# A four-layer graph network: rows of edge weights fed to TensorE between windows, and layer 1 regrouped as 6, 7, 6, 6

## The chip, the cores and the metric

The kernel runs on one core of a Trainium2 chip. The metric is the device time of one execution in microseconds; the time of the kernel before is the median of three runs.

## The reference

A graph of 3125 nodes with 128 features and 103,125 edges sorted by destination goes through four layers, each followed by a residual and a layer norm. Cut to what the change touches, layers 0 and 1:

```python
# layer 0: weighted sum over edges
xw = x @ weight
out = relu(segment_sum(edge_val[:, None] * xw[src], dst, N) + b)
x = layernorm(x + out)

# layer 1: four heads of attention over the edges, and a loop on each node
h = (x @ W).reshape(n, 4, 32)
e = leaky_relu(a_s[src] + a_d[dst], 0.2)
p = exp(e - segment_max(e, dst)[dst])
out = segment_sum(h[src] * (p / z[dst])[:, :, None], dst, n)   # z = segment_sum(p, dst)
out = layernorm_with_gain(out.reshape(n, 128) + gat_bias + x @ skip_W + skip_b)
x = layernorm(x + out)
```

Layer 2 is an attention over the edges with one head, layer 3 two mean aggregates with matrices. Both read the counts of edges that the first stage makes.

## The kernel before, in words

The edges are turned into two dense matrices in device memory once: `wd`, the sums of edge weights (float32, source by destination, read by rows), and `f_ctd`, the counts of edges (bf16, read by all later layers). The nodes are 25 blocks of 128, the sums over edges then matrix products. Only `fast_path` runs here; a general path stands behind a flag.

*Edge stage (`make` L827, loop L871 to L931).* The edges are cut into windows of 5 nodes each; 16 windows make a batch of 80 nodes, and there are 40 batches, of which the last has 4 windows. For the next batch VectorE makes the one-hot matrices `ohd` and `ohc` (L849) and the weighted `wod` (L860, the weight in three bf16 parts); ScalarE makes part of the third (`more`, L866). For each four windows of the batch TensorE then makes 8 products of counts (`cp`, L893) and 24 of weights (`wp`, L901) in two PSUM tiles of a three-bank pool (tag "cw"); ScalarE copies them out to `cs` (L906) and `ws` (L912), with four of its own scalings for the next batch between (`cur[3](k)`). At the batch's end SyncE issues two stores of `ws` to `wd` (L914), after every odd batch one of `cs` to `f_ctd` (L917).

*Keys (`keys_of` L659).* Every eighth batch (b % 8 == 2, while batches 8 to 32 are ahead) the edges' columns are turned by six TensorE transposes into two tiles of the same three banks, and copies by ScalarE and VectorE (L537, L539, L694, L697, L698) spread them from there; the banks are held until the last has read them.

*Rows of layer 0 (`add0` L801, `while` L927).* After batch 2, whenever a row block of 128 sources is complete in `wd` by stores a batch older, SyncE issues two loads of half a row, 640 KB each (`cw`, L807, pool `f_zp` of three tiles), and TensorE runs 20 float32 products of it (L811) into five PSUM banks that hold the first 20 destination blocks. Rows that aren't done at the end of the loop follow after it (L930). A scheduler orders each engine's instructions over the whole stage, by its own costs and the priorities of the source's order; nothing is fixed by hand.

*Before layer 1 (L1188 to L1209).* The remaining five destination blocks are summed from all 25 rows (pool `tp`), and between the rows stand the attention scores of the first 20 blocks (`scores1`), their factors, and every third row from row 13 on the values of two blocks (`values`, L1158 on).

*Layer 1 (L1198 to L1349).* The destinations are taken in groups of blocks, `IG` (L503), with two heads at a time; such a sweep goes over the 25 chunks of sources. A chunk's counts are loaded, and two masks are made: one in five by VectorE alone (L1249), the others by ScalarE (`fm`, L1255) and VectorE (`cm`, L1256). For each block of the group TensorE runs three products (L1266, L1271) into the block's own PSUM bank. After a sweep VectorE sums the parts (`sums`, L1290), GpSimd and VectorE form the quotients (L1296 to L1312). Other work is hung between the chunks by `later` and `step`: the skip products (`skips`, L1276 to L1280), norms (`finish1`, L1039), the turned features for layer 2 (`turn2`, L1009 to L1020). They take their PSUM tile from `bank()`, which is one bank named "few" here, beside seven banks for the group's blocks. In group 0 other work is hung as well: the scores and factors of blocks 20 to 24 and the rest of the values.

Of the kernel before, what the change touches and what calls it, by code (L numbers as in the profile page):

```python
# [7 lines left out]
F32 = mybir.dt.float32  # L8
# [493 lines left out]
GM = 40.0  # L502
IG = [(0, 4), (4, 7), (11, 7), (18, 7)]  # L503
QG = [(0, 13), (13, 12)]
# [6 lines left out]
def fast_path(  # L511
# [146 lines left out]

    def keys_of(g):  # L659

        eg = egs[g]
        kd2 = kp.tile([P, P // BW, 2, BW, 2], BF16, name="kd2")
        kc2 = kp.tile([P, P // BW, 2, BW, 2], BF16, name="kc2")
        w2 = [kp.tile([P, P // BW, 2, BW, 2], BF16, name=f"w2_{s}") for s in range(3)]
        kic = ep.tile([P, EW], F32, name="kic", bufs=2)
# [5 lines left out]
        kid = ep.tile([P, EW], F32, name="kid", bufs=2)  # L671
        nc.vector.tensor_copy(kid.rearrange("p (a k) -> p a k", k=16), eg[:, :, 1, :])
        wei = ep.tile([P, EW], F32, name="wei", bufs=2)
# [12 lines left out]
        def pairs(i, h):  # L686
            return each(i, h)[:, :, :, None].to_broadcast([P, P // BW, BW, 2])

        wt = ep.tile([P, 2, P], F32, name="wt", bufs=2)
        wu = kp.tile([P, 2, P], F32, name="wu")  # L690
        for h in range(2):
            copy(kd2[:, :, h, :, :], pairs(t0, h))
            copy(kc2[:, :, h, :, :], pairs(t0[:, 2:, :], h))
            nc.scalar.copy(w2[0][:, :, h, :, :], pairs(t1, h))  # L694
        for s, (i, o) in enumerate(((t1, wt), (wt, wu))):
# [6 lines left out]
    keys = {0: keys_of(0)}  # L702


# [55 lines left out]
    def xw_of(b0, n):  # L760

        t = zps.tile([P, 512], F32, name="trx", tag="acc0")
        for k in range(n):
            nc.tensor.transpose(t[:, k * P : (k + 1) * P], x[:, b0 + k, :], ident)
        xT = ep.tile([P, 512], F32, name="f_xTb", bufs=2)
        nc.scalar.copy(xT[:, : n * P], t[:, : n * P])
# [33 lines left out]

    def add0(pool, i, accs, blocks):  # L801

        b0, n = blocks
        for h in range(0, n, 10):
            m = min(10, n - h)
            cw = pool.tile([P, min(10, n), P], F32, name="cw")[:, 0:m]
            nc.sync.dma_start(  # L807
                cw.rearrange("p c d -> p (c d)"), wd[i * P : (i + 1) * P, (b0 + h) * P : (b0 + h + m) * P]
            )
# [61 lines left out]
    acc0 = None  # L871
    done = 0
    cur = make(0)
    with tc.issue_after(tip[0].ins), tc.issue_after(tip["keys"].ins):
        keys[1] = keys_of(1)
    for k in range(0, BW, 4):
        cur[3](k)
    for b in range(NBT):
# [8 lines left out]
        for k in range(0, nw, 4):  # L887
# [22 lines left out]
            if cur and (b + 1 < NBT - 1 or k < LW):  # L910
                cur[3](k)
            nc.scalar.copy(ws[:, k : k + 4, :], wp)  # L912
        for a, e in ((0, 112), (112, KW)):
            nc.sync.dma_start(wv_[b * BW : b * BW + nw, a:e, :].rearrange("w k d -> k w d"), ws[a:e, 0:nw, :])  # L914
# [6 lines left out]
        if b == 2:  # L921
# [158 lines left out]
    with ExitStack() as st:  # L1080
# [29 lines left out]
        def scores1(g):  # L1110

            b0, n = GB[g]
            tag = f"acc{min(g, 2)}"
            turned(zps, xT, b0, n, tag)
            for k in range(n):
                b = b0 + k
                nc.tensor.matmul(
                    t8[:, b * 2 * H : (b + 1) * 2 * H], xT[:, b * P : (b + 1) * P], watt, start=True, stop=True
                )
            t = zps.tile([P, 512], F32, name="tr_ad", tag=tag)  # L1120
            nc.tensor.matmul(t[0:H, : n * P], watt[:, H:], xT[:, b0 * P : (b0 + n) * P], start=True, stop=True)
# [3 lines left out]

        def heads(b0, n):

            b = slice(b0, b0 + n)
            nc.vector.tensor_copy(
                sa[:, b, :], t8[:, b0 * 2 * H : (b0 + n) * 2 * H].rearrange("p (b h) -> p b h", h=2 * H)  # L1130
            )
            nc.vector.tensor_scalar(nas[:, b], sa[:, b, 0:H], -1.0, None, OP.mult)
            nc.gpsimd.tensor_scalar(bas[:, b], sa[:, b, 0:H], UP, None, OP.mult)
# [48 lines left out]
        def top():  # L1182
            heads(0, Z0)
            ex = fp.tile([P, H], F32, name="ex", bufs=1)
# [99 lines left out]
        def sums(acc, g, hp):  # L1284
# [462 lines left out]
```

## Time and profile before

| what | us |
|---|---|
| median of three runs (1521.67 to 1522.70) | 1522.51 |
| the profiled execution | 1520.03 |
| its span in the profile | 1518.2 |
| edge stage with rows, 90.0 to 467.5 | 377.5 |
| rows left after it, 467.5 to 500.0 | 32.5 |
| last five blocks of layer 0 and scores, 500.0 to 543.5 | 43.5 |
| layer 1, 543.5 to 953.5, four groups in two sweeps each | 410.0 |
| layer 1's end and layer 2, to 1249 | 295.5 |
| layer 3, to 1518.2 | 269.2 |

The profiled execution is 1.83 us longer than its span, and 2.48 shorter than the median. In the profile's lines an engine is PE (TensorE), PEld (its weight loads), DVE (VectorE), ACT (ScalarE), POOL (GpSimd) or SP (SyncE); "SPq" is SyncE's issuing. A row of the table by stage reads: from:to and length, then for each engine its busy time and, in brackets, its instructions, then TensorE's granted clock as a share of full speed, the busy share of the 16 DMA engines, and the rate in GB/s. A row of waits reads: the engine, what waits and at which line, what released it, the total in us, how often, and the longest. A group of instructions reads: line, engine, operation, result and operands with their shapes, how many; then busy time in us and the mean of one in ns; then idle time just before them and what ended it. Ends of products are modelled, so the step from one product's start to the next one's is the safer measure of its cost.

### The profile page before, as it was taken

The page shows a single profiled execution, that of the slowest core. Times are in us where ns is not written, and L with a number is a line of the kernel's source. Part 1 is how long each engine was busy: PE and PEld are TensorE (multiplying, and loading weights), DVE is VectorE, ACT ScalarE, POOL GpSimd, SP SyncE. Part 2 cuts the span into 40 slices and gives each one's busy share as a digit, 9 for nine tenths or more (in the row PEclk, how much of TensorE's full clock was granted, in tenths as well). Part 3 has the DMA queues.
Part 4 walks back from the last instruction along what each step waited for, and adds up shares of the span by engine and source line. Part 5 has one row for each costly group of instructions (what it writes and reads, how often), then busy time and mean ns, then how long its engine had stood idle before and what let it go on. Part 6 is the DMA issues. An engine that isn't in the chain of part 4 may idle for free. (4 is left out here: it accounts for less than half of the span.)

```text
span 1518.2 us, 35039 instructions
## 1 busy us (share of the span) xinstructions
PE 1386.5 (91%) x14762; PEld 1214.1 (80%) x14775; DVE 979.0 (64%) x1619; ACT 905.9 (60%) x1847; POOL 129.9 (9%) x163
## 2 busy tenths in 40 slices
PE   4898999999998987899989989899999999999995
PEld 3798999899898876889979979677777774458995
DVE  4999999989990489879968878544465352012006
ACT  2988887878882479878778677454465331023003
POOL 1000000000000023203212311300000000000000
PEclk9999999999999999999999999999999999999997
DMA  7378887877889633444434433332222218513541
GB/s 204 93 182 230 217 221 191 245 196 207 230 229 254 214 93 98 144 124 123 129 116 120 130 92 105 119 115 68 69 60 80 76 58 301 197 43 131 197 154 46
DMA packets 209734, 223.92 MB, mean 147 GB/s; under 512 B 72988, under 2 KB 183371, under 8 KB 209309
## 3 DMA queue, kind: packets, MB, share of 16 engines
q1 hardware_dynamic: 208780, 218.51, 49.7%
q8 instruction: 117, 1.92, 0.5%
q0 software_dynamic: 400, 1.97, 0.4%
q10 hardware_dynamic: 385, 1.11, 0.2%
q14 instruction: 52, 0.43, 0.1%
HBM read 157.19 MB, written 64.36 MB: 146 GB/s over the span
## 5 line engine op out<-in xcount | busy, mean ns | idle before, releaser
L1271 PE MATMUL acc<-vp,cm 128*128 128x198 bf16 x2500 | 343.0, 251 | 7.3 <-DVE cm L1256 4.6
L1255 ACT ACTIVATE fm<-adr,bas 128x896 bf16<-128x896 f32 (+1 forms) x320 | 286.2, 952 | 68.1 <-DVE cm L1256 63.5
L1266 PE MATMUL acc<-vp,ct 128*128 128x204 bf16 x1250 | 314.2, 255 | 9.9 <-DVE vp L1174 5.6
L1271 PEld LDWEIGHTS <-cm 128*128 128x128 bf16 x2500 | 234.9, 98 | 27.1 <-issue 10.1
L901 PE MATMUL wp<-wod,ohc 128*128 128x128 bf16 x3768 | 239.1, 219 | 7.1 <-ACT cs L906 7.1
L901 PEld LDWEIGHTS <-ohc 128*128 128x128 bf16 x3768 | 220.0, 98 | 8.2 <-issue 7.8
L1256 DVE TENSOR_TENSOR cm<-fm,ct 128x896 bf16<-128x896 bf16 (+1 forms) x320 | 198.3, 650 | 36.3 <-PE acc L1271 14.8
L860 DVE TENSOR_TENSOR wod<-ohd,w 128x4096 bf16<-128x4096 bf16 (+2 forms) x122 | 221.1, 1867 | 0.6 <-PE wp L901 0.6
L866 ACT ACTIVATE wod<-ohd,wu 128x128 bf16<-128x128 bf16 x628 | 192.8, 398 | 0.0
L1411 DVE TENSOR_TENSOR e<-e,ct 128x416 f32<-128x416 f32 (+1 forms) x175 | 108.3, 625 | 106.5 <-ACT e L1410 99.2
L1410 ACT ACTIVATE e<-s,f_nm 128x416 f32<-128x416 f32 (+1 forms) x175 | 109.6, 633 | 98.1 <-PE s L1407 91.0
L1415 PEld LDWEIGHTS acc<-self__8020,e 128*128 128x128 f32 x1250 | 148.2, 193 | 20.6 <-issue 18.8
L1415 PE MATMUL acc<-self__8020,e 128*128 128x129 f32 x1250 | 148.6, 276 | 0.6 <-DVE e L1411 0.6
L1407 PE MATMUL s<-yT,f_xT 128*128 128x416 f32 (+1 forms) x350 | 142.8, 543 | 4.6 <-ACT rt L1387 4.0
L811 PE MATMUL acc<-f_xw,cw 128*128 128x128 f32 x1000 | 120.0, 280 | 5.7 <-DMA cw<-wd 5.7
L1266 PEld LDWEIGHTS <-ct 128*128 128x128 bf16 x1250 | 122.2, 98 | 2.5 <-issue 1.5
L811 PEld LDWEIGHTS acc<-f_xw,cw 128*128 128x128 f32 x1000 | 116.4, 196 | 6.3 <-DMA cw<-wd 6.3
L912 ACT COPY ws<-wp 128x512 f32<-128x512 f32 x157 | 91.8, 585 | 48.1 <-PE wp L901 46.7
L893 PE MATMUL cp<-ohc,ohd 128*128 128x125 bf16 x1256 | 95.7, 218 | 23.5 <-ACT ws L912 19.3
L1407 PEld LDWEIGHTS s<-yT,f_xT 128*128 128x128 f32 x350 | 62.2, 191 | 55.5 <-issue 39.4
L849 DVE TENSOR_TENSOR ohd<-kd,ramp 128x4096 bf16<-128x4096 bf16 (+1 forms) x41 | 90.0, 2198 | 23.5 <-PE cp L893 23.5
L893 PEld LDWEIGHTS <-ohd 128*128 128x128 bf16 x1256 | 78.2, 98 | 28.8 <-issue 28.7
(303 smaller groups left out, 1521.3 us busy)
## 6 DMA issues: line engine op xcount, KB each, us to landing
ct<-f_ctd SPq DMA_DIRECT2D x46, 800.0 KB
wd<-ws SPq DMA_DIRECT2D x39, 896.0 KB
ct<-f_ctd SPq DMA_DIRECT2D x150, 224.0 KB
cw<-wd SPq DMA_DIRECT2D x50, 640.0 KB
f_ctd<-cs SPq DMA_DIRECT2D x20, 1000.0 KB
ct<-f_ctd SPq DMA_DIRECT2D x25, 416.0 KB
ct<-f_ctd SPq DMA_DIRECT2D x25, 365.2 KB
cw<-wd SPq DMA_DIRECT2D x25, 320.0 KB
```

Of the source, the lines that this page charges most:

```text
L811: nc.tensor.matmul(accs[j // 4][:, j % 4, :], cw[:, j - h, :], xw[:, i, :], start=False, stop=(i == NB - 1 and (j % 4 == 3 or j == n - 1)) ...
L860: tip[s] = nc.vector.tensor_tensor(packed(f, ww), packed(ohd, ww), twos(w2[s])[:, ww], OP.mult)
L866: nc.scalar.activation(wod[2][:, BW + w, :], ohd[:, BW + w, :], AF.Copy, scale=w3[:, 1, at : at + 1])
L893: nc.tensor.matmul(cp[:, j, 0:KW], ohd[:, w, :], ohc[:, w, 0:KW], start=(j == 0 and q == 0), stop=(j == 3 and q == 1), skip_group_check=True,)
L901: made = nc.tensor.matmul(wp[:, j, :], ohc[:, w, :], wod[s][:, w, :], start=(j == 0 and q == 0 and s == 0), stop=(j == 3 and q == 1 and s ...
L1255: nc.scalar.activation(f[:, : n * P], at, AF.Relu, bias=bas[:, c, h : h + 1], scale=UP)
L1256: nc.vector.tensor_tensor(m[:, : n * P], f[:, : n * P], ct[:, : n * P], OP.min)
L1266: nc.tensor.matmul(out_(F1, PW), ct[:, k * P : (k + 1) * P], vp[:, c, hp : hp + 2, :, 2 * F1 : V1], start=(c == 0), stop=False, skip_group ...
L1271: nc.tensor.matmul(out_(0, 2 * F1)[:, j], ms[j][:, k * P : (k + 1) * P], vp[:, c, hp + j, :, 0 : 2 * F1], start=False, stop=(c == NB - 1 a ...
L1407: nc.tensor.matmul(s[:, :m], xT[:, c * P : (c + 1) * P], yT[:, i0 * P + a : i0 * P + a + m], start=True, stop=True)
L1410: nc.scalar.activation(e[:, a : a + m], s[:, :m], AF.Exp, bias=nm[:, q : q + 1], scale=scale)
L1415: nc.tensor.matmul(acc[k // 3][:, (k % 3) * (P + 1) : (k % 3 + 1) * (P + 1)], es[q, c][:, k * P : (k + 1) * P], vo[:, c, 0 : P + 1], start ...
```

## The change

*Keys.* `keys_of` is cut in two. `columns_of(g)` (at b % 8 == 1) makes the columns, `keys_of(kid, kic, wei)` (at b % 8 == 3) the six transposes; each of its two PSUM tiles is now copied by ScalarE at once to SBUF (`k_`, `w_`), and the spreading copies read those. The small tiles of the pool `ep` have one buffer instead of two.

*Rows.* `adds0` issues the loads of a row and returns its 20 products as steps; `add0` runs them at once, as before. From batch 3 on, TensorE and SyncE keep the order of the source (`tc.manual_schedule`), to the loop's end. After each four windows 3, 4, 3 and 3 steps are run from the list `todo`. The next row is loaded there as soon as at most 20 steps are listed and the row is complete: by the stores up to batch b−2 in the first half of batch b, by those up to b−1 in its second half. The pool for rows has four tiles (two rows) instead of three.

*Layer 1.* The groups are 6, 7, 6, 6 blocks instead of 4, 7, 7, 7. Group 0 takes its six banks from `acc3`, `acc4`, `acc2`, `tr_sa`, `left0`, `left1`; scores of blocks 20 to 24 use `acc1` and `acc0` and make their `heads` inside `scores1`. Values stand at every odd row from 13 on, six pairs instead of four, and so seven instead of nine remain for group 0. In groups 1 to 3 `bank()` alternates between "few" and the seventh accumulator's bank where the group has six blocks. Group 0's quotients come 7 steps after its sums instead of 4.

```diff
-IG = [(0, 4), (4, 7), (11, 7), (18, 7)]
+IG = [(0, 6), (6, 7), (13, 6), (19, 6)]
...
+    def keys_of(kid, kic, wei):
+
         kd2 = kp.tile([P, P // BW, 2, BW, 2], BF16, name="kd2")
...
-        t0 = cps.tile([P, 4, P], F32, name="t0", tag="cw")
-        t1 = cps.tile([P, 2, P], F32, name="t1", tag="cw")
+        k_ = ep.tile([P, 4, P], BF16, name="k_")
+        w_ = ep.tile([P, 2, P], F32, name="w_")
+        t = cps.tile([P, 4, P], F32, name="t", tag="cw")
         for h in range(2):
-            a = slice(h * P, (h + 1) * P)
-            nc.tensor.transpose(t0[:, h, :], kid[:, a], ident)
-            nc.tensor.transpose(t0[:, 2 + h, :], kic[:, a], ident)
-            nc.tensor.transpose(t1[:, h, :], wei[:, a], ident)
+            nc.tensor.transpose(t[:, h, :], kid[:, h * P : (h + 1) * P], ident)
+            nc.tensor.transpose(t[:, 2 + h, :], kic[:, h * P : (h + 1) * P], ident)
+        nc.scalar.copy(k_, t)
+        t = cps.tile([P, 4, P], F32, name="t", tag="cw")
+        for h in range(2):
+            nc.tensor.transpose(t[:, h, :], wei[:, h * P : (h + 1) * P], ident)
+        nc.scalar.copy(w_, t[:, 0:2, :])
...
-    def add0(pool, i, accs, blocks):
+    def adds0(pool, i, accs, blocks):
 
         b0, n = blocks
+        steps = []
         for h in range(0, n, 10):
...
             for j in range(h, h + m):
-                nc.tensor.matmul(
-                    accs[j // 4][:, j % 4, :], cw[:, j - h, :], xw[:, i, :], start=False,
+                steps.append(lambda j=j, a=cw[:, j - h, :]: nc.tensor.matmul(
+                    accs[j // 4][:, j % 4, :], a, xw[:, i, :], start=False,
                     stop=(i == NB - 1 and (j % 4 == 3 or j == n - 1)), skip_group_check=True,
-                )
+                ))
+        return steps
...
-    zp = front.enter_context(tc.tile_pool(name="f_zp", bufs=3))
+    zp = front.enter_context(tc.tile_pool(name="f_zp", bufs=4))
...
-        if b % 8 == 2 and 8 < b < NBT - 8:
-            keys[b // 8 + 1] = keys_of(b // 8 + 1)
+        if b % 8 == 1 and 8 < b < NBT - 8:
+            keys[b // 8 + 1] = columns_of(b // 8 + 1)
+        if b % 8 == 3 and 8 < b < NBT - 8:
+            keys[b // 8 + 1] = keys_of(*keys[b // 8 + 1])
...
             nc.scalar.copy(ws[:, k : k + 4, :], wp)
+            if order:
+                m = min(4 if k == 4 else 3, len(todo))
+                for f in todo[:m]:
+                    f()
+                del todo[:m]
+
+                if len(todo) <= 20 and (done + 1) * P <= (b - (k < 8)) * BW * WN:
+                    todo += adds0(zp, done, acc0, (0, Z0))
+                    done += 1
...
-        while acc0 and (done + 1) * P <= (b - 1) * BW * WN:
-            add0(zp, done, acc0, (0, Z0))
-            done += 1
+
+            order = ExitStack()
+            order.enter_context(tc.manual_schedule(engines={mybir.EngineType.PE, mybir.EngineType.SP}))
+    order.close()
+    for f in todo:
+        f()
     for i in range(done, NB):
         add0(zp, i, acc0, (0, Z0))
...
-            if i >= 13 and i % 3 == 1:
+            if i >= 13 and i % 2:
                 values(ready)
                 ready += 2
...
-        later(7, lambda: (heads(Z0, NB - Z0), factors(Z0, NB - Z0)))
+        later(7, lambda: factors(Z0, NB - Z0))
...
-            later(1 if last else 4, quotients)
+            later(1 if last else 4 if g else 7, quotients)
...
-                spare.append(lambda: ap.tile([P, 512], F32, name="few"))
+                turn = [0]
+
+                def few():
+
+                    turn[0] ^= len(acc) < 7
+                    return ap.tile([P, 512], F32, name="acc1_6" if turn[0] else "few")
+
+                spare.append(few)
             if c == 0:
                 if g == 0:
-                    acc = [zps.tile([P, 512], F32, name="acc1", tag=f"acc{3 + k}") for k in range(2)]
-                    acc += [zpp.tile([P, 512], F32, name="acc1", tag=f"left{k}") for k in range(2)]
+                    acc = [zps.tile([P, 512], F32, name="acc1", tag=f"acc{k}") for k in (3, 4, 2)]
+                    acc += [zpp.tile([P, 512], F32, name="acc1", tag=k) for k in ("tr_sa", "left0", "left1")]
```

More of the change, by code (lines that the diff above doesn't have):

```diff
@@ L657, in fast_path, with columns_of @@
     nc.sync.dma_start(x[0:NR, NF, :], x_in[NF * P : N, :])
-    def keys_of(g):
+    def columns_of(g):
         eg = egs[g]
[L662 to L665, printed above, removed]
+        kic = ep.tile([P, EW], F32, name="kic")
         nc.vector.tensor_scalar(
@@ L670, in keys_of @@
         nc.vector.memset(kic[:, EW - 1 : EW], -1.0)
-        kid = ep.tile([P, EW], F32, name="kid", bufs=2)
+        kid = ep.tile([P, EW], F32, name="kid")
         nc.vector.tensor_copy(kid.rearrange("p (a k) -> p a k", k=16), eg[:, :, 1, :])
-        wei = ep.tile([P, EW], F32, name="wei", bufs=2)
+        wei = ep.tile([P, EW], F32, name="wei")
         nc.scalar.copy(wei.rearrange("p (a k) -> p a k", k=16), eg[:, :, 2, :])
-        t0 = cps.tile([P, 4, P], F32, name="t0", tag="cw")
-        t1 = cps.tile([P, 2, P], F32, name="t1", tag="cw")
-        for h in range(2):
-            a = slice(h * P, (h + 1) * P)
-            nc.tensor.transpose(t0[:, h, :], kid[:, a], ident)
-            nc.tensor.transpose(t0[:, 2 + h, :], kic[:, a], ident)
-            nc.tensor.transpose(t1[:, h, :], wei[:, a], ident)
+        return kid, kic, wei
+    def keys_of(kid, kic, wei):
+        kd2 = kp.tile([P, P // BW, 2, BW, 2], BF16, name="kd2")
+        kc2 = kp.tile([P, P // BW, 2, BW, 2], BF16, name="kc2")
+        w2 = [kp.tile([P, P // BW, 2, BW, 2], BF16, name=f"w2_{s}") for s in range(3)]
+        k_ = ep.tile([P, 4, P], BF16, name="k_")
+        w_ = ep.tile([P, 2, P], F32, name="w_")
+        t = cps.tile([P, 4, P], F32, name="t", tag="cw")
+        for h in range(2):
+            nc.tensor.transpose(t[:, h, :], kid[:, h * P : (h + 1) * P], ident)
[5 more added lines that the diff above has]
+        nc.scalar.copy(w_, t[:, 0:2, :])
         def each(i, h):
@@ L687, in pairs @@
             return each(i, h)[:, :, :, None].to_broadcast([P, P // BW, BW, 2])
-        wt = ep.tile([P, 2, P], F32, name="wt", bufs=2)
+        wt = ep.tile([P, 2, P], F32, name="wt")
         wu = kp.tile([P, 2, P], F32, name="wu")
         for h in range(2):
[L692 to L695, printed above, removed]
+            copy(kd2[:, :, h, :, :], pairs(k_, h))
+            copy(kc2[:, :, h, :, :], pairs(k_[:, 2:, :], h))
+            nc.scalar.copy(w2[0][:, :, h, :, :], pairs(w_, h))
+        for s, (i, o) in enumerate(((w_, wt), (wt, wu))):
             for h in range(2):
@@ L701, in fast_path @@
     tip = {}
-    keys = {0: keys_of(0)}
+    keys = {0: keys_of(*columns_of(0))}
     l0_wt = cst.tile([P, P], F32, name="f_l0_wt")
@@ L764, in xw_of @@
             nc.tensor.transpose(t[:, k * P : (k + 1) * P], x[:, b0 + k, :], ident)
-        xT = ep.tile([P, 512], F32, name="f_xTb", bufs=2)
+        xT = ep.tile([P, 512], F32, name="f_xTb")
         nc.scalar.copy(xT[:, : n * P], t[:, : n * P])
@@ L810, in add0 @@
             for j in range(h, h + m):
-                nc.tensor.matmul(
-                    accs[j // 4][:, j % 4, :], cw[:, j - h, :], xw[:, i, :], start=False,
+                steps.append(lambda j=j, a=cw[:, j - h, :]: nc.tensor.matmul(
+                    accs[j // 4][:, j % 4, :], a, xw[:, i, :], start=False,
                     stop=(i == NB - 1 and (j % 4 == 3 or j == n - 1)), skip_group_check=True,
-                )
+                ))
+        return steps
+    def add0(*args):
+        for f in adds0(*args):
+            f()
     def end0(acc, b0, n):
@@ L872, in fast_path @@
     done = 0
+    todo = []
+    order = None
     cur = make(0)
     with tc.issue_after(tip[0].ins), tc.issue_after(tip["keys"].ins):
-        keys[1] = keys_of(1)
+        keys[1] = keys_of(*columns_of(1))
     for k in range(0, BW, 4):
@@ L926, in fast_path @@
                 bias0(a, 4)
-        while acc0 and (done + 1) * P <= (b - 1) * BW * WN:
-            add0(zp, done, acc0, (0, Z0))
-            done += 1
+            order = ExitStack()
+            order.enter_context(tc.manual_schedule(engines={mybir.EngineType.PE, mybir.EngineType.SP}))
+    order.close()
+    for f in todo:
+        f()
     for i in range(done, NB):
@@ L1112, in scores1 @@
             b0, n = GB[g]
-            tag = f"acc{min(g, 2)}"
+            tag = f"acc{min(g, 2) if b0 < Z0 else 1}"
             turned(zps, xT, b0, n, tag)
+            t, a = (t8, b0) if b0 < Z0 else (zps.tile([P, 512], F32, name="tr_s", tag="acc0"), 0)
             for k in range(n):
-                b = b0 + k
                 nc.tensor.matmul(
-                    t8[:, b * 2 * H : (b + 1) * 2 * H], xT[:, b * P : (b + 1) * P], watt, start=True, stop=True
-                )
+                    t[:, (a + k) * 2 * H : (a + k + 1) * 2 * H], xT[:, (b0 + k) * P : (b0 + k + 1) * P], watt,
+                    start=True, stop=True,
+                )
+            if b0 >= Z0:
+                heads(t, b0, n)
             t = zps.tile([P, 512], F32, name="tr_ad", tag=tag)
@@ L1124, in scores1, with heads @@
             nc.sync.dma_start(add_[:, b0 * P : (b0 + n) * P], ad[:, : n * P])
-        def heads(b0, n):
+        def heads(t, b0, n):
             b = slice(b0, b0 + n)
-            nc.vector.tensor_copy(
-                sa[:, b, :], t8[:, b0 * 2 * H : (b0 + n) * 2 * H].rearrange("p (b h) -> p b h", h=2 * H)
-            )
+            nc.vector.tensor_copy(sa[:, b, :], t[:, 0 : n * 2 * H].rearrange("p (b h) -> p b h", h=2 * H))
             nc.vector.tensor_scalar(nas[:, b], sa[:, b, 0:H], -1.0, None, OP.mult)
@@ L1182, in top @@
         def top():
-            heads(0, Z0)
+            heads(t8, 0, Z0)
             ex = fp.tile([P, H], F32, name="ex", bufs=1)
```

## The prediction

> **What bounds the kernel now.** I read the page first, then a table of busy times by stage, then the waits and stretches of the timeline inside the stages that the change touches.
>
> ```profile
> span 1518.2 us, 35039 instructions
> PE 1386.5 (91%) x14762; PEld 1214.1 (80%) x14775; DVE 979.0 (64%) x1619; ACT 905.9 (60%) x1847; POOL 129.9 (9%) x163
> ```
>
> TensorE is busy for 91% of the span, so there are at most some 130 us of its idle time to win, and any new wait of TensorE is paid in full. The stages (start:end, length, busy time of each engine, granted clock, DMA share, GB/s):
>
> ```profile
> core 0: us, PE busy (x) PEld busy (x) DVE busy (x) ACT busy (x) POOL busy (x), PEclk, DMA share, GB/s
> 90.00:467.50 377.50, 351.86 (x5328) 346.77 (x5326) 344.33 (x203) 310.28 (x852) 1.35 (x1) 1.00 0.81 216
> 467.50:500.00 32.50, 24.92 (x182) 23.29 (x180) 5.72 (x33) 4.95 (x11) 1.45 (x2) 0.89 0.85 253
> ...
> 543.50:594.50 51.00, 38.72 (x351) 32.26 (x352) 47.73 (x140) 48.33 (x90) 13.43 (x25) 0.97 0.30 87
> 594.50:624.90 30.40, 28.08 (x308) 26.81 (x307) 27.24 (x68) 26.97 (x41) 5.38 (x7) 1.00 0.45 133
> 624.90:682.90 58.00, 50.98 (x531) 48.90 (x531) 43.73 (x93) 47.20 (x65) 11.71 (x11) 0.97 0.44 129
> 682.90:729.40 46.50, 45.69 (x520) 45.34 (x518) 41.42 (x60) 37.34 (x40) 11.91 (x7) 1.00 0.48 133
> 729.40:791.40 62.00, 54.08 (x557) 50.97 (x555) 49.88 (x109) 46.94 (x68) 15.24 (x10) 0.97 0.39 118
> 791.40:840.00 48.60, 47.54 (x535) 46.87 (x532) 43.25 (x64) 38.37 (x47) 11.33 (x8) 1.00 0.45 128
> ```
>
> The first row is the edge stage with the row products, the second the rows left after it. The six below are layer 1's groups 0, 1 and 2, two head pairs ("sweeps") each; group 3 takes 61.8 and 51.7. Group 0's first sweep isn't TensorE's (38.7 of 51.0) but ScalarE's and VectorE's (48.3, 47.7); the others are TensorE's with waits.
>
> What TensorE waits for in the edge stage, first row, and in layer 1, second and third (engine, line, releaser, total us, times, longest):
>
> ```profile
> PE cp L893 <- ACT ws L912: 17.9, 14, 1.6
> ```
>
> ```profile
> PE few L1279 <- DVE f_xw L1280: 10.3, 7, 3.4
> PE few L1014 <- ACT f_x L1005: 5.8, 2, 2.9
> ```
>
> TensorE's steps for four windows, and SyncE's issues at the end of a batch (start, length):
>
> ```profile
> 250.57 1.50 PE L901 MATMUL wp<-wod,ohc 128*128 128x128 bf16 x24
> 251.91 0.60 PE L893 MATMUL cp<-ohc,ohd 128*128 128x125 bf16 x8
> ```
>
> ```profile
> 242.03 1.98 SPq L914 DMA_DIRECT2D wd<-ws  x2
> 244.07 1.65 SPq L917 DMA_DIRECT2D f_ctd<-cs  x1
> 245.82 5.42 SPq L807 DMA_DIRECT2D cw<-wd  x2
> ```
>
> Start to start, 24 weight products take 1.34 us and 8 counts 0.44 (252.35 − 251.91): 1.78 per four windows, 7.12 per batch. Forty row products (two rows) take 4.68 less their step to the next group, so 0.226 each, 4.52 a row. Eight batches, five rows and the key transposes (0.67) are 57.0 + 22.6 + 0.7 = 80.2 us; the trace has batch ends 88.3 apart (144.53, 232.82, 321.12). So 8.1 us per eight batches are waits; summed from batch 2's end (73.6) to batch 39's (467.5), 33.5. VectorE has 82.1 us of work in such 88.3, ScalarE 72.5. The row weights that a load at 245.82 fetched landed at 255.4 by the semaphore records, 13.4 after the store's issue at 242.03; a store (512-byte packets) lands 5.5 after its issue, and a row load with nothing ahead of it 4.0 to 5.5 after its own.
>
> **What the Trainium skill says.** "DMA: Bandwidth & Descriptors", § Two DMAs through the same engine are not ordered: a transfer that reads what another wrote must wait, at its issuing engine, for the first one's completion. So SyncE must hold a row load until the store before it has landed. Before, no load meets this: it reads stores a batch older. "TensorE: Matmul & The Clock Gate", § HAM oscillation, warns of gaps of TensorE over about 3.4 us, after which the clock is halved. The trace agrees on the halving and is stricter on the gap. In the first of these stretches a wait of 2.30 us (L1279 for L1280's read, up to 740.12) stands:
>
> ```profile
> 738.00:741.40 3.40, 1.28 (x13) 1.27 (x14) 3.40 (x5) 2.94 (x3) 0.96 (x2) 1.00 0.23 67
> 741.40:744.90 3.50, 3.50 (x23) 3.13 (x22) 3.41 (x9) 3.21 (x4) 2.12 (x2) 0.51 0.23 59
> ```
>
> The 3.4 us after it run at 0.51: up to 1.7 us lost, some 1.3 where the engine would have waited anyway.
>
> **The change part by part.**
>
> *TensorE in source order, rows spread (edge stage).* Instead of one lump of 20 or 40 products, each four windows are followed by 3, 4, 3, 3. TensorE then needs 80.2 / 32 = 2.51 us per four windows, ScalarE 2.27, VectorE 2.57: nobody is late by much, and ScalarE empties the banks meanwhile. The waits of before go: −33.5. What is late next is the row itself.
>
> *Weight rows loaded mid-batch (SyncE in source order).* A batch makes 80 of 128 nodes of a row, 12.5 products; 13 are taken, so the list runs dry. Where the next row needs batch b−1, its load stands in the program after window 8 of batch b, and its first product after window 12. Counted through the program, at that slot the list holds at most two older products for b = 4, 12, 20, 28, 36 and 10, 18, 26, 34 (b−1 odd, so a count store lies ahead) and 7, 15, 23, 31 (b−1 even). Need: four times 1.78 plus 9 to 13 row products, and the transposes where they fall: 9.2 to 11.7 us after the end of batch b−1. Supply: the store is issued 0.8 to 1.25 after the batch's end (0.8 in before where ScalarE ends with cs and ws, 3.8 where window scalings stand between; the new order on ScalarE keeps them apart). Behind a count store the row lands 13.4 later, so at 14.2 to 14.6; else 5.5 + 4.75, at 11. Waits: five of 4.7 to 5.1 (the first 3.8), three of 2.2 to 2.6, one of 3.3, four of 0.5 to 0.9, and 0.6 at the start: 34.8 us with 0.8, 40.7 with 1.25. I take 36. Both ends of the landing: 11 everywhere (counts don't hold the load back) gives about 12; 1 us later than taken gives 49. Queued behind SyncE's wait are only the next batch's stores, not due for 5 us; behind TensorE's are all products of the batch, while VectorE and ScalarE stop a batch ahead for lack of buffers. So the wait isn't made up.
>
> *Clock.* Nine waits exceed 2 us; the six longest are sure to leave over 2 us of one of the page's free-running 3.4-us windows idle. Six times 1.3, and a share of the three: +8 (0 if none; 13 at the most). In before this stage ran at 1.00.
>
> *Left after the edges.* By the same count 452 of 500 row products lie inside, 48 after, against 420 and 80: moved, not saved. The 10 us of waits of that tail (32.5 less 80 × 0.226 and its slow clock) depend on the last store, which stays: 0. Edges: −33.5 + 36 + 8 = +10.5.
>
> *Keys in two parts.* Same six transposes. Two more ScalarE copies out of PSUM (0.58 each, as L912's) per eight batches lie in ScalarE's 15.8 idle us; without that cover 1.2 each time. The 1.5 us of waits on L697 are in the sum above. The two at the start: −0.7 (−1.5 to +1).
>
> *Values and scores.* Two more value pairs before layer 1, with VectorE, ScalarE at 20 of 43.5 us busy there and TensorE at 42.3: some 1 us of TensorE's, +1 (0 to 3). The matching gain is in the next part.
>
> *Groups 6, 7, 6, 6.* A mask of n blocks costs ScalarE 711 ns at n = 4 and 1032 at n = 7:
>
> ```profile
> L1255 ACT ACTIVATE fm<-adr,bas 128x896 bf16<-128x896 f32 x240 | 233.8, 1032 | 64.9 <-DVE cm L1256 60.4 <-DVE mv L993 3.4 <-DVE ms L1003 0.9
> L1255 ACT ACTIVATE fm<-adr,bas 128x512 bf16<-128x512 f32 x80 | 52.4, 711 | 3.1 <-DVE cm L1256 3.0
> ```
>
> So 107 per block, 925 at 6; on VectorE 626 (436 and 721) and 1086 (787 and 1236). TensorE: 0.26 us per block and chunk, 25 chunks: 26, 39, 45.5. The blocks sum to 25 either way. Group 0's first sweep: ScalarE 48.3 + 40 × 0.214 = 56.9, VectorE 47.7 + 40 × 0.19 + 10 × 0.30 − 3 for the values = 55.3, TensorE 38.7 + 13 = 51.7: all near 56.5, with 13 us more of products inside. Second: 30.4 + 13 less 1.4 of idle time, 42. Group 1 keeps its size: 60 (it inherits more norms) and 46.5. Groups 2 and 3 at 6: 62 and 61.8 less 6.5 of products, less a seventh of the rest's 9, less bank waits 2: 52.5 and 51.5; then 42 and 44. Sum 395 against 410: −15. Bounds: −20, and −3, where ScalarE (37 of 39 us of products in a 6-wide sweep, against 41 of 45.5) makes itself felt.
>
> *Two small banks.* The skips wait 10.3 us for VectorE to read the only bank, the turns 5.8; two banks break this for 6-wide groups. It is the 2 us a sweep above. Fewer such chains where layer 1 ends: −1.5.
>
> Sum: +10.5 − 0.7 + 1 − 15 − 1.5 = −5.7. The profiled run took 1520.03 (1.83 around the span), giving 1514.3; the median shown is 2.5 above that run: 1516.8, so 1517.
>
> **The rivals.** *Rows arrive in time.* For: DMA engines are busy 0.81, not full. Against: 13.4 us were measured behind counts. Waits 12, none over 2 us, so no clock loss: edges −21.5, sum −37.7, 1485; halfway to the forecast 1501. I place it at 1492.
>
> *Slower: each late row is dearer.* SyncE issues the two halves only after the landing, and they took it 5.42 us; if rows land 1 us later than taken, 13 rows cost 13 more and the clock 2 more: edges +25.5, layer 1 −12: +12, 1535. It decides from 5.7 / 13 = 0.45 us later. Against: half loads overlap the count store's 4.8 us.
>
> *Layer 1 doesn't gain.* 6-wide sweeps turn ScalarE's: −3 there, sum +6, 1529; in its milder form 1524. For: 37 of 39. Against: five masks may wait ahead.
>
> **How the numbers follow.** This kernel's measurement can tell about 0.2%, 3 us: same is 1519.5 to 1525.5. Forecast 0.48 (1509 to 1524; faster 0.37, same 0.11), in time 0.17 (faster), dearer 0.23 (slower), no gain 0.12 (same 0.03, slower 0.09). Faster 0.54, same 0.14, slower 0.32. The range 1494 to 1536 leaves out half of the second case and a third of the third.
>
> **What would show it.** Right: in the edge stage waits of a row product on its load, some 5 us long at every eighth batch, a clock of 0.5 after each, and no more waits on L912; sweeps of groups 2 and 3 near 52 and 42. Wrong: these waits under 1 us (second case), or 6-wide sweeps over 43 us in their second half (fourth). If the clock stays at 1.00, 8 us come off.

## The result, and the profile after

The changed kernel takes 1548.82 us (median of four runs, 1546.55 to 1551.59) against 1522.61 before (four runs too): a ratio of 1.0171, interval 1.0152 to 1.0189. It is slower, where 5.7 us less were forecast, and lies above the forecast's range of 1494 to 1536. The page of its profiled execution, 1546.55 us:

```profile
span 1544.8 us, 35055 instructions
PE 1401.4 (91%) x14775; PEld 1231.5 (80%) x14775; DVE 984.4 (64%) x1621; ACT 915.5 (59%) x1857; POOL 128.8 (8%) x164
...
PEclk9999999999999799999999999999999999999998
```

TensorE's busy share is still 91%, but busy time itself grew by 15 us with the same products: a first sign of a slower clock, which the last line (the clock in 40 slices) shows for slice 14, where the rows after the loop run (7 for seven tenths). The table by stage, in the columns of before; first the edge stage and the rows after it, then the sweeps of groups 0, 1 and 2:

```profile
core 0: us, PE busy (x) PEld busy (x) DVE busy (x) ACT busy (x) POOL busy (x), PEclk, DMA share, GB/s
90.00:500.50 410.50, 373.12 (x5396) 367.84 (x5393) 345.86 (x202) 318.18 (x861) 1.35 (x1) 0.97 0.77 205
500.50:524.50 24.00, 14.08 (x102) 13.89 (x100) 1.95 (x13) 1.87 (x2) 1.45 (x2) 0.72 0.67 197
...
574.00:634.00 60.00, 50.99 (x497) 46.30 (x498) 54.24 (x135) 56.52 (x87) 11.30 (x22) 0.94 0.39 115
634.00:676.20 42.20, 39.91 (x442) 38.93 (x441) 38.20 (x73) 35.70 (x42) 7.94 (x7) 1.00 0.43 122
676.20:734.80 58.60, 51.95 (x547) 49.74 (x544) 50.36 (x102) 47.62 (x65) 14.18 (x10) 0.97 0.42 125
734.80:785.30 50.50, 48.06 (x532) 47.04 (x532) 43.23 (x64) 38.04 (x48) 10.34 (x8) 1.00 0.42 119
785.30:842.00 56.70, 47.48 (x484) 44.57 (x482) 47.27 (x107) 42.22 (x68) 14.28 (x10) 0.94 0.38 109
842.00:887.30 45.30, 41.71 (x464) 40.74 (x462) 38.97 (x69) 34.77 (x48) 9.93 (x8) 1.00 0.41 116
```

The edge stage is 33 us longer, its clock 0.97 instead of 1.00; VectorE has about the same work in it, ScalarE some 8 us more. TensorE's waits in it, from batch 2's end on, and SyncE's before it issues row loads (first 490 us):

```profile
PE acc L820 <- DMA cw<-wd: 34.8, 12, 5.3
PE cp L911 <- ACT ws L930: 2.4, 3, 0.8
```

```profile
SPq L816 <- DMA wd<-ws: 62.7, 24, 5.0
```

Where before the copies of ScalarE held TensorE (17.9 us on L912), now row products hold it, waiting for their own load (12 waits); and SyncE, before it issues such a load, waits for the store to land. One such place, TensorE and SyncE side by side, around the end of batch 20 (start, length, and in brackets the wait just before; a float32 product leaves two entries, 1000 for the 500 of this stage, so x6 is three products):

```profile
278.39 1.50 PE L919 MATMUL wp<-wod,ohc 128*128 128x128 bf16 x24
285.24 1.65 PE L820 MATMUL acc<-f_xw,cw 128*128 128x128 f32 x6 [5.34 <-DMA cw<-wd]
286.68 1.05 PE L911 MATMUL cp<-ohc,ohd 128*128 128x125 bf16 x8
287.52 2.77 PE L919 MATMUL wp<-wod,ohc 128*128 128x128 bf16 x24
```

```profile
271.25 2.34 SPq L941 DMA_DIRECT2D wd<-ws  x2
273.64 1.40 SPq L944 DMA_DIRECT2D f_ctd<-cs  x1
276.83 3.59 SPq L816 DMA_DIRECT2D cw<-wd  x2
```

The weights' store goes out at 271.25, the counts' at 273.64, the row load only at 276.83, after the weights have landed. The row's first half arrives at 285.2, 14.0 after the store's issue. After the wait the 24 products take 2.77 us instead of 1.50. The granted clock of the two stretches, the third figure from the right, says why (1.00, then 0.50):

```profile
276.00:284.60 8.60, 3.90 (x68) 3.71 (x66) 8.60 (x6) 8.60 (x28) 0.00 (x0) 1.00 1.03 263
284.60:291.40 6.80, 6.17 (x44) 6.10 (x45) 4.75 (x3) 3.18 (x9) 0.00 (x0) 0.50 0.71 199
```

Cut at instructions (batch 2's and the last weight product, the last row product of the first 20 blocks, the last of the other five, and the first sum after each sweep), the spans compare like this; "inside" counts the row products before the loop's end:

| us | before | after | difference | forecast |
|---|---|---|---|---|
| to batch 2's end | 73.6 | 74.9 | +1.3 | -0.7 |
| loop, inside: 420 and 449 | 393.8 | 425.5 | +31.7 | |
| rows after the loop | 29.2 | 25.5 | -3.7 | +10.5 with the loop |
| last five blocks, scores, values | 44.5 | 47.0 | +2.5 | +1 |
| layer 1, eight sweeps | 412.4 | 409.0 | -3.4 | -15 |
| behind it | 564.7 | 562.9 | -1.8 | -1.5 |

The sum is +26.6, the difference of the spans. The loop with its rows is off by 17.5 us and layer 1 by 11.6; the other lines by 2 or less.

### The profile page after: what moved, and what is told of

It is laid out like the page before. It is cut to its first block, busy times and chain, and to the rows that moved or that the text cites. A ratio compares the mean times of both kernels' runs of the same rounds, so it can differ in the third digit from the quotient of the medians.

```text
span 1544.8 us, 35055 instructions
## 1 busy us (share of the span) xinstructions
PE 1401.4 (91%) x14775; PEld 1231.5 (80%) x14775; DVE 984.4 (64%) x1621; ACT 915.5 (59%) x1857; POOL 128.8 (8%) x164
## 4 chain that ended last, share of the span: by engine, by line
PE 70%; DVE 9%; DMA 9%; ACT 8%; issue 2%; POOL 2%; SPq 0%; DVEq 0%; ACTq 0%; POOLq 0%
PE wp L919 9%; PE acc L1302 9%; PE acc L1453 9%; PE s L1445 8%; PE acc L1553 6%; PE acc L820 6%; PE acc L1629 6%; DMA cw<-wd 5%; PE acc L1297 5%; DVE cm L1287 3%; PE cp L911 3%; ACT wod L882 3%; PE left L820 2%; DMA wd<-ws 1%; ACT fm L1286 1%
## 5 line engine op out<-in xcount | busy, mean ns | idle before, releaser
L1297 PE MATMUL acc<-vp,ct 128*128 128x204 bf16 x1250 | 317.1, 255 | 10.2 <-DVE vp L1205 4.5
L1286 ACT ACTIVATE fm<-adr,bas 128x768 bf16<-128x768 f32 (+1 forms) x320 | 287.3, 953 | 61.9 <-DVE cm L1287 60.0
L1287 DVE TENSOR_TENSOR cm<-fm,ct 128x768 bf16<-128x768 bf16 (+1 forms) x320 | 202.9, 666 | 29.0 <-PE acc L1302 14.7
L882 ACT ACTIVATE wod<-ohd,wu 128x128 bf16<-128x128 bf16 x628 | 197.4, 399 | 0.0
L820 PE MATMUL acc<-f_xw,cw 128*128 128x128 f32 x1000 | 152.3, 294 | 44.8 <-DMA cw<-wd 44.7
L820 PEld LDWEIGHTS acc<-f_xw,cw 128*128 128x128 f32 x1000 | 130.4, 201 | 47.3 <-DMA cw<-wd 47.3
L924 ACT CAST cs<-cp 128x500 bf16<-128x500 f32 x157 | 90.4, 576 | 47.6 <-PE cp L911 46.6
L1445 PEld LDWEIGHTS s<-yT,f_xT 128*128 128x128 f32 x350 | 62.4, 191 | 55.4 <-issue 40.7
```

The costliest lines, as they stand in the source:

```text
L820: steps.append(lambda j=j, a=cw[:, j - h, :]: nc.tensor.matmul(accs[j // 4][:, j % 4, :], a, xw[:, i, :], start=False, stop=(i == NB - 1 a ...
L882: nc.scalar.activation(wod[2][:, BW + w, :], ohd[:, BW + w, :], AF.Copy, scale=w3[:, 1, at : at + 1])
L1286: nc.scalar.activation(f[:, : n * P], at, AF.Relu, bias=bas[:, c, h : h + 1], scale=UP)
L1287: nc.vector.tensor_tensor(m[:, : n * P], f[:, : n * P], ct[:, : n * P], OP.min)
L1297: nc.tensor.matmul(out_(F1, PW), ct[:, k * P : (k + 1) * P], vp[:, c, hp : hp + 2, :, 2 * F1 : V1], start=(c == 0), stop=False, skip_group ...
L1445: nc.tensor.matmul(s[:, :m], xT[:, c * P : (c + 1) * P], yT[:, i0 * P + a : i0 * P + a + m], start=True, stop=True)
```

## The experiments

My theory after this trace: the edge stage carries the whole loss, by rows that come late. Rivals: the fixed order and the cut-up rows are the loss; layer 1's groups are part of it. All medians below are beside runs of the kernel before on the same chip (1523.1 to 1524.4), and ratios with their intervals are to those; the change's own 1549 was measured beside 1522.6, so a difference to it can carry some 2 us of that. Diffs are to the changed kernel in the runs on the edge stage and to layer 1's part alone in the last three.

**The two halves of the change alone.** The kernel before with the hunks of the edge stage (`edges_only`) or those of layer 1, values and scores (`layer1_only`).

> The kernel before with the change's edge stage alone (keys, source order, rows between the windows); layer 1 and the values as before. Theory (the edge stage carries the whole loss): its end came 27 us later in the changed kernel's trace, so +27 us on before, about 1550. Rival (layer 1's groups carry a good part, hidden by the stage cuts): +15 or less, under 1538.

Measured: 1551.31, ratio 1.0177 (1.0151 to 1.0204). Its loop takes 425.8, its rows after it 24.6, layer 1 412.2.

> The kernel before with groups of 6, 7, 6, 6, the two small banks and the moved values and scores alone; edges as before. Theory from the changed kernel's trace: +5 before layer 1 and -4 to -6 in it and behind it, 0 to -2 in all, about 1521. Rival (the sweeps suffered from what the edge stage left behind and gain by themselves as forecast): -10 to -15, about 1510.

Measured: 1520.46, ratio 0.9975 (0.9964 to 0.9986): some 4 us faster by the medians, 1.4 by the two traces' spans. Its loop takes 393.8 and layer 1 410.2. So the edge stage carries all of the loss, and layer 1's part gains 1 to 4 us by itself: it isn't that the edge stage spoils it.

**Older stores.** The row is loaded one batch later.

```diff
-                if len(todo) <= 20 and (done + 1) * P <= (b - (k < 8)) * BW * WN:
+                if len(todo) <= 20 and (done + 1) * P <= (b - 1) * BW * WN:
```

> The changed kernel, with one edit: a row is loaded only when the stores two batches back complete it, in both halves of a batch, so that SyncE has nothing to wait for. Theory (the fresh store is the cause): the 34.8 us of row waits in the edge stage and some 12 us of halved clock go, about 3 us come back as one more half row after the loop: 1549 - 44 = 1505. Rival (the fixed order of TensorE and SyncE and the cut-up rows are the cause): 1535 or more.

Measured: 1638.16, ratio 1.0742 (1.0716 to 1.0767). My theory missed it by 133 us. The rival's bound holds, but what holds TensorE is again the rows. Its waits in the loop:

```profile
PE acc L820 <- DMA cw<-wd: 105.3, 18, 8.5
```

SyncE waits almost nowhere for a store here (once, 3.3 us), and yet the rows come later still. The trace shows it at 239.15: the load is issued as the third thing after the batch's two kinds of store, and its first product stands one group of windows later, 2.5 us in the program:

```profile
235.44 1.95 SPq L941 DMA_DIRECT2D wd<-ws  x2
237.44 1.60 SPq L944 DMA_DIRECT2D f_ctd<-cs  x1
239.15 6.40 SPq L816 DMA_DIRECT2D cw<-wd  x2
```

So the wait for a fresh store is not needed for a late row: the load, issued behind a whole batch's stores, has too little work between itself and its first product. The clock is halved for 122.9 us of its loop. This changed my theory to: what is late is a load with too little work ahead of its use; the counts ahead of it in the queues make the worst of it. The next two runs test these two parts.

**Counts behind the row load.** The store of counts is kept back (`held`) and issued after the third group of the next batch.

```diff
+                if k == 8 and held:
+                    nc.sync.dma_start(*held.pop())
...
-            nc.sync.dma_start(ctd[:, :, i0 : i0 + SB * BW * WN].rearrange("c d i -> d c i"), cs)
+            held.append((ctd[:, :, i0 : i0 + SB * BW * WN].rearrange("c d i -> d c i"), cs))
+            if not order or b == NBT - 1:
+                nc.sync.dma_start(*held.pop())
```

> The changed kernel, with one edit: the store of counts is issued in the next batch after its third group of four windows, behind the row load there instead of ahead of it. Theory (a row load lands late because the counts lie ahead of it in the queues): the long waits fall from 5.3 to some 1.7 us, those of 1.5 go, the halved clock goes: -25 to -30, about 1521. Rival (the wait for the store's landing is the most of it, whatever lies ahead): -8 or less.

Measured: 1512.83, ratio 0.9915 (0.9887 to 0.9942): 36 us less than the changed kernel, and faster than before. SyncE waits longer for stores than in the change (77.1 us against 55.2, both from 75 to 470), so that wait isn't what made the rows as late as they were. TensorE's row waits in the loop:

```profile
PE acc L820 <- DMA cw<-wd: 10.4, 10, 1.7
```

They fall by 24.4 us and none is over 1.7, and no stretch of the loop has a halved clock, against 27.3 us of such stretches in the change (up to half of it lost). The loop is 36.0 shorter (389.5).

**A reserve in the list.** Thirteen products always stay, so that a row has a batch to arrive.

```diff
-                m = min(4 if k == 4 else 3, len(todo))
+                m = min(4 if k == 4 else 3, max(0, len(todo) - 13))
```

> The changed kernel, with one edit: 13 row products (a batch's worth) always stay in the list, so that the first product of a newly loaded row comes a batch after its load instead of one group of four windows after it; loads, stores and their order are as in the change. Theory (the list runs dry, so each load is awaited at once): no row waits above 1 us in the edge stage, no halved clock there, and the 13 products kept to the end fill a wait that stands there already: 1549 - 35 - 12 = 1502, within 6. Rival (the fixed order and the order of the queues set it): 1535 or more.

Measured: 1516.32, ratio 0.9953 (0.9941 to 0.9965). The direction holds, the size doesn't: 32 us of the 47. No row waits are left in the loop, but others have come:

```profile
PE wp L919 <- ACT cs L924: 14.0, 10, 2.9
PE wp L919 <- ACT ws L930: 2.3, 4, 1.0
```

The longest, 2.7 to 2.9 us, stand in the batches with the key transposes (at 158.75, 247.34, 336.50), where ScalarE has ten more copies to make; these batches take 15.8 to 16.0 us, and 10.2 us of the loop run at half clock. One would think that TensorE's row waits had given ScalarE the time for these copies. But in the run `fixed_rows` below, without row loads, there are no row waits, and a key batch takes 12.1 us, as in the change. What differs is the order in which ScalarE does its work, which the scheduler chose anew for each build. With the reserve, the copy that TensorE waits for stands behind eight scalings (seven here, the eighth at 246.44):

```profile
244.08 2.15 ACT L882 ACTIVATE wod<-ohd,wu 128x128 bf16<-128x128 bf16 x7
246.74 0.55 ACT L924 CAST cs<-cp 128x500 bf16<-128x500 f32 x1
247.34 2.10 PE L919 MATMUL wp<-wod,ohc 128*128 128x128 bf16 x24 [2.69 <-ACT cs L924]
```

In `fixed_rows`, at the same place, the copies come first:

```profile
237.47 0.58 ACT L937 COPY ws<-wp 128x512 f32<-128x512 f32 x1
237.94 0.57 ACT L931 CAST cs<-cp 128x500 bf16<-128x500 f32 x1
240.07 2.44 ACT L889 ACTIVATE wod<-ohd,wu 128x128 bf16<-128x128 bf16 x8
```

No run puts the one order into the other kernel, so what the order costs as a whole isn't measured.

**The rows in one lump.** As the reserve, but all 13 products after the batch's last four windows.

```diff
-                m = min(4 if k == 4 else 3, len(todo))
+                m = min(13 if k == 12 else 0, max(0, len(todo) - 13))
```

> As the run with 13 products in reserve, but the 13 products of a batch stand in one lump after its last four windows instead of 3, 4, 3, 3. Theory (spreading the rows is what took away the waits for ScalarE's copies): the waits for these copies come back, 0.9 us a batch, less the 0.18 a batch that cutting the rows up costs: 25 us slower than with the rows spread, about 1527. Rival (the fixed order alone takes them away, or the slack of the lump makes up for them): within 6 of the spread version.

Measured: 1520.59, ratio 0.9982 (0.9974 to 0.9990). It is 4 us slower than with the rows spread, not 25, so the rival's bound holds. It doesn't settle what takes the waits for ScalarE's copies away: they are 21.2 us here, but 18.5 with the rows spread, and were 22.1 before. Neither reserve run is rid of them, and both have another order on ScalarE than the change.

**No rows to wait for.** Each later row uses the first one's weights, its own load is left out.

```diff
-            cw = pool.tile([P, min(10, n), P], F32, name="cw")[:, 0:m]
...
+            if b0 == 0 and h in first_row:
+                cw = first_row[h]
+            else:
+                cw = pool.tile([P, min(10, n), P], F32, name="cw")[:, 0:m]
...
+                    first_row[h] = cw
```

> The changed kernel, with the row loads of the first 20 destination blocks left out, all but those of the first row: its weights are used for every row, so layer 0's sums are not the reference's; all products, stores and their order stay. Theory (what the edge stage is without any wait for rows): the loop takes 378 us instead of 425.5 and the wait of 9.9 after it goes: 1549 - 48 - 10 = 1491. Rival (without the row waits ScalarE comes late at the key batches, as in the run with a reserve): the loop takes 388 to 396, so 1502 to 1510.

Measured: 1481.98, ratio 0.9725 (0.9709 to 0.9742). The loop takes 375.9 and the rows after it 11.4; the rival (ScalarE late at the keys) isn't seen. It is 9 us below the theory: 4 of them are the rows after the loop, where the clock now stays whole too, and 2 the loop. Without their loads the queues are also emptier (DMA share 0.66 instead of 0.77), so this is the case of rows that lie ready and cost no transfer. Its stage, and TensorE's longest waits in the loop:

```profile
90.00:451.00 361.00, 358.56 (x5398) 356.12 (x5396) 345.41 (x202) 313.97 (x861) 1.35 (x1) 1.00 0.66 153
```

```profile
PE cp L918 <- ACT ws L937: 2.4, 3, 0.8
```

This is the edge stage of the change without late rows: TensorE is busy 358.6 of 361.0 us, beside VectorE with 345.4. Loop and rows after it are 387.3 together, 63.7 below the change. The fixed order and the cut-up rows are all there, and the kernel is 41 us faster than before: the first rival, that they are the loss, is out.

**Counts and reserve together.** The kernel with the counts moved, a reserve of 6 instead of none (`both`), and then also the last counts' store behind the last row loads (`both_tail`). The diff is to the run with the counts moved.

```diff
-                m = min(4 if k == 4 else 3, len(todo))
+                m = min(4 if k == 4 else 3, max(0, len(todo) - 6))
...
-            if not order or b == NBT - 1:
+            if not order:
...
     for i in range(done, NB):
         add0(zp, i, acc0, (0, Z0))
+    nc.sync.dma_start(*held.pop())
```

> The changed kernel with the counts stored behind the row load, and 6 products kept in the list. Theory (the waits of up to 2 us that are left with the counts moved go with a small reserve): the loop takes 380 us, 1503. Rival (ScalarE's key copies take their place, as with the reserve of 13): no faster than 1512.

Measured: 1508.44, ratio 0.9904 (0.9888 to 0.9921). The loop takes 386.2, with no row waits in it but 11.2 us for ScalarE's copies; between the two expectations.

> As the run before, and the last store of counts is issued behind the last rows' loads instead of ahead of them. Theory: the 9.2 us wait after the loop is partly for these counts, so 4 us less than the run before. Rival (it is the last weight store's own landing): within 1, or slower because layer 1 waits for the counts.

Measured: 1503.59, ratio 0.9874 (0.9858 to 0.9890), the fastest of the versions that compute what the reference asks for. The wait for the last rows falls from 8.3 us to

```profile
PE acc L820 <- DMA cw<-wd: 4.2, 1, 4.2
```

and the rows after the loop from 23.9 to 19.9: as expected, half of this wait was for the counts. Loop and rows are 406.2 here, 17 below before.

**Layer 1: a later norm.** GpSimd's three steps between a group's two norms take 6.6 us for 7 blocks; here they get eight chunks instead of five.

```diff
-                    later(1 if last else 3, lambda: finish1(ends[-1], g, (1, 1) if last else (1, 5)))
+                    later(1 if last else 3, lambda: finish1(ends[-1], g, (1, 1) if last else (1, 8)))
```

> The kernel before with layer 1's part alone, and one edit: the second norm of a group starts 8 chunks after the first one's scaling instead of 5. Theory (GpSimd's three steps between the norms, 6.6 us for 7 blocks, no longer fit into five chunks of a 6-wide group, so that VectorE and then TensorE's turns wait): -4 to -6 against the same without the edit, in the first sweep of group 2. Rival (that sweep is ScalarE's and VectorE's): within 1.

Measured: 1522.07, ratio 0.9998 (0.9985 to 1.0011), so not faster than the 1520.46 without the edit. The first sweep of group 2 falls from 57.6 to 54.1, its wait of 5.9 us for the norm is gone, but group 1's second sweep grows from 50.8 to 55.5, since group 0's turns are pushed into it. The wait was real; the time only moved.

**Layer 1: one small bank.**

```diff
-                    turn[0] ^= len(acc) < 7
+                    turn[0] = 0
```

> The kernel before with layer 1's part alone, and one edit: the small tiles of groups 2 and 3 all use one bank, as before the change. Theory (the second bank is worth what the waits of the skips and turns before were): +4 to +6 against the same with two banks. Rival (the waits only move to the next releaser): within 1.5.

Measured: 1518.84, ratio 0.9975 (0.9965 to 0.9985), the same ratio as with two. The second bank is worth nothing that these runs can tell.

**Layer 1: fewer masks in group 0.**

```diff
+                if g == 0 and c % 5 in (1, 2, 3) and h > hp and (2 * c + h) % 5:
+                    ms.append(ms[0])
+                    continue
```

> The kernel before with layer 1's part alone, and 10 of 50 masks of each of group 0's two sweeps left out (a second head takes the first one's mask), so that layer 1's sums are not the reference's there: ScalarE has 9.3 us less, VectorE 6.3, TensorE the same. Theory (group 0's first sweep is ScalarE's and VectorE's at 6 blocks too): it falls from 59.7 to about 53, the second by 1 at most. Rival (its waits are those of the values' chain and of loads): it falls by less than 2.

Measured: 1516.97, ratio 0.9955 (0.9938 to 0.9971). The first sweep falls from 59.7 to 55.4, the second stays (42.3 and 42.8). So group 0's first sweep is in part ScalarE's and VectorE's at six blocks too, by 4.3 us. Of TensorE's 9.3 us of idle time in it 7.0 stay without these masks: the waits for VectorE's part of the values fall from 4.5 to 1.5, one of 2.6 for a load of counts stays.

## Why the prediction was wrong

It had the mechanism of the loss, late rows and a slower clock after them, and still forecast a gain: in the edge stage the clock and the tail were priced too low and the gain too high, and layer 1's gain wasn't there. By its own steps:

*Row waits, 36: right in sum.* The trace has 34.8, in twelve waits. Long ones were forecast for batches 12, 20, 28 and 36 at 4.7 to 5.1: 5.33, 5.34, 5.24 and 4.58 were measured; those of the key batches at 2.2 to 2.6: 1.3 to 1.6; the first 3.8: 3.3. One missed is 2.45 in batch 31, forecast below 0.9. So the sum is as near as it is partly because errors cancel. That the counts ahead of the load make the long ones is shown by moving the counts.

*The clock, +8, at the most 13: the first step that failed in the edge stage.* From the run without rows to wait for, the change is 63.7 us longer in the loop and the rows after it; the row waits are 34.8 and, after the loop, 9.9; what is left, 19.0, I put down to the halved clock. The trace has 27.3 us of it in the loop and 13.7 after, of which half can be lost, 20.5: they agree. The kernel before lost up to 3.4 of the kind after its loop, so the change added some 15.6 where 8 were forecast. I took 3.4 us of half clock after each wait, from a wait of 2.3 us in layer 1; after two of the three waits over 5 us it lasted 6.8. The page "TensorE: Matmul & The Clock Gate" of the Trainium skill, § Part 1: The HAM clock gate, says that a busy window brings the clock back and that windows run free, of 3.4 us each; the traces agree, as the last section shows. In the place shown above the half clock begins at 284.6, 0.65 us before the wait's end, so that this window isn't wholly busy, and the next runs at half as well; at the wait of 5.33 it is 0.45, and the clock is back after one. For the rows after the loop I counted nothing, though the clock there was at half for 13.7 us against 6.8 before.

*Rows left after the loop, 0: missed by 3.5.* TensorE's waits there are 9.9 against 6.4 before. In the run `both` this wait is 8.3, and 4.2 once the last counts go behind the loads.

*Removing 33.5 us of waits: right in kind, short by 8.* Without waits for rows, and without the 10 us of waits and slow clock after the loop, loop and rows would have been 423.0 - 33.5 - 10 = 379.5; measured 387.3. Three or four float32 products between bf16 ones cost more than in a lump: a batch of 13 takes 10.24 in that run's trace, where 7.12 + 13 × 0.226 is 10.06, so 0.18 a batch and 6.5 in 36. Waits for ScalarE's copies are 2.4 there; the two are 8.9, a little more than what is missing. (The 33.5 was itself a remainder; the trace of before has 23.6 us of waits from 90 to 467. And where the prediction reads x40 as forty products and two rows, it is one row's 20; its 0.226 each and 4.52 a row are right.) The reason given for the gain, that rows between the windows give ScalarE its time, isn't shown: spread or in one lump, the two runs with a reserve keep most of the waits. That ScalarE's idle 15.8 us per eight batches cover the key copies held in the order that ScalarE had in the change, up to a wait of 0.8 each; in the order of the reserve run it didn't, by up to 2.9.

Against the forecast these terms are +7.6 for the clock, +3.5 for the waits after the loop, +7.8 for the gain and -1.2 for the row waits, which comes to the 17.5 within 0.2.

*Groups 6, 7, 6, 6 with two banks, -15: the step that failed in layer 1.* Layer 1 came 3.4 shorter; the change's part alone, 2.2. The masks were priced well (926 ns for six blocks where 925 was forecast):

```profile
L1286 ACT ACTIVATE fm<-adr,bas 128x768 bf16<-128x768 f32 x240 | 209.1, 926 | 42.6 <-DVE cm L1287 41.8 <-DVE ms L1033 0.4
```

What failed is what a sweep makes of them. TensorE's idle time over the eight sweeps was 42.9 us and is 40.7, its half clock 17.1 and is 23.9: the idle time that was to be filled has stayed. For group 0 I set the first sweep equal to ScalarE's busy time, 56.5; before, ScalarE had been busy 48.3 of 51.0 us, and now it is 56.5 of 60.0: a bound engine wasn't full before either. Group 1's second sweep was to stay at 46.5 and takes 50.5, with turned features in it that before stood elsewhere, and a wait of 2.3 at one of them. For group 2 I took waits off and forecast 52.5 and 42; it takes 56.7 and 45.3. The norm of group 1's seven blocks came too late for chunks that had become shorter (a wait of 5.9, and 6.8 us of half clock), and the maximum over the first 13 blocks moved from group 3's last sweep into group 2's second (two waits of 1.5). The "layer 1 doesn't gain" rival, at -3, was the true case of this part. Its reason, that 6-wide sweeps turn ScalarE's, isn't seen: its sign, over 43 us in a second sweep, came in group 2 alone, and there ScalarE is busy for 34.8 of 45.3 us; the second sweeps of groups 2 and 3 wait 3.6 and 0.7 us only.

*Values before layer 1, +1:* 2.5, but the run `edges_only`, with the values of before, is 3.2 longer there as well: no more values are needed for it. All versions but the run without row loads have 3.4 or 6.8 us of half clock in this stretch, and before has none. *Start, -0.7:* +1.3, and nothing can be read from it: the runs on layer 1's part, whose start is that of before, reach batch 2's end between 72.9 and 76.4.

*The rivals.* "Each late row is dearer" was the case that came, at 1535 for 1549: its sign and place were right, its mechanism only in part: the rows were hardly later than taken (14.0 for 13.4), the clock after them was dearer. What stays open: why group 0's first sweep keeps 7 us of idle time without the masks, what ScalarE's order costs, and whether another spacing of the hung work would bring layer 1 the forecast gain; none was tried further.

## What to carry to other kernels

Before a load is moved closer to its source, count the work that stands in program order between the load and its first use, and the transfers queued ahead of it: here a group of windows (2.5 us) faced 14 us, and six products of reserve with the counts' store moved behind turned 1549 into 1508. Price an idle gap of TensorE with the clock after it: a 5.3-us gap cost up to 3.4 more. When an edit changes what one engine's list holds, look at the order that the scheduler gives the others: with a reserve, ScalarE's order changed, and a key batch went from 12.1 us to 15.8. And when group sizes change, don't set a stage to its bound engine's busy time; use the share that this engine reached before (48.3 of 51.0 here, 56.5 of 60.0 after).

## What the runs showed of the hardware

In the changed kernel's loop the clock stayed whole after row waits of up to 1.6 us and after one of 3.31; it was halved for 3.4 us after waits of 2.45, 3.22, 4.58 and 5.33, and for 6.8 after those of 5.34 and 5.24. So the length of a wait alone doesn't set the price. Where it falls does. In each of the fourteen traces all changes of the clock lie multiples of 3.41 us apart. Cut into such windows, the loops of these traces show: after a window at full clock in which TensorE was idle for 1.83 us or less the clock stayed, in all 1555 cases; after one with 2.02 or more it was halved, in all 36. The wait of 3.31 lies across two windows, idle for 1.51 and 1.80; the wait of 2.45 puts 2.18 into one (busy 1.90, 1.61 and 1.23 us):

```profile
96.86:100.27 3.41, 1.90 (x34) 1.72 (x31) 3.21 (x3) 3.40 (x11) 0.00 (x0) 1.00 1.04 232
100.27:103.68 3.41, 1.61 (x22) 1.60 (x23) 3.41 (x2) 3.11 (x11) 0.00 (x0) 1.00 1.00 362
410.88:414.29 3.41, 1.23 (x20) 1.04 (x16) 3.41 (x2) 2.04 (x6) 0.00 (x0) 1.00 0.77 294
414.29:417.71 3.42, 3.15 (x25) 3.09 (x26) 3.42 (x3) 0.57 (x1) 0.00 (x0) 0.50 1.02 260
```

Once halved, the clock came back after windows with up to 0.51 us of idle time and stayed halved after those with 0.68 or more; of two cases between, 0.65 stayed and 0.66 came back. This holds for the loop; behind the rows, where products of 8 columns stand, less idle time was enough (0.79 in the change). In the run with older stores, 18 waits of 5.9 us in the mean go with 122.9 us of half clock, 6.8 each in the mean.
